# Where the sum of squares of a gated norm is issued: out of the output product, in between the next piece's products

## The chip, the core and the metric

The kernel runs on one core of a Trainium2 chip. Its engines are named as the profile names them: TensorE (PE, with its weight loads PEld), VectorE (DVE), ScalarE (ACT), GpSimd (POOL) and SyncE (SP). Each engine takes its instructions in the order in which the kernel issues them, and waits at an instruction until what it reads is there. The metric is the device time in microseconds of one execution.

## The reference

The input is 4 sequences of 1024 rows by 512. Four blocks are added to it, one after the other: a mixer ("a": 16 heads of 64, state 64), a feed-forward block, a second mixer ("b": 64 heads of 16, state 128), and the feed-forward block again with the same weights. Each block reads a layer-normalised copy of x. A mixer is a state-space layer:

```
proj = norm(x) @ in_proj            # z (1024), h (1024), B, C, dt (one per head)
h, B, C = silu(conv4(h, B, C))      # causal convolution, 4 taps
dt = softplus(dt + bias); decay per head = exp(dt * A)
y  = scan over time (state <- state*decay + dt*h*B; y = C.state) + D*h
a:  yf = y * silu(z);  out = (norm_w * yf * rsqrt(mean(yf^2) + eps)) @ out_proj
b:  out = (norm_w * y * rsqrt(mean(y^2) + eps) * silu(z)) @ out_proj
```

What matters here is the last line of each: the mean of 1024 squares for each row gives one factor a row. That factor commutes with the output product, so it can be put on the product's 512 outputs.

## The kernel before, in words

The kernel runs mixer a, the feed-forward block, mixer b and the feed-forward block in sequence. Within a mixer the rows are tiled by 128 (a chunk, 8 to a sequence), and two chunks form a group (256 rows); 16 groups follow each other. Matrix products are float32, and each is issued to PE as two passes, so that the profile counts each twice.

Two kinds of work are interleaved by hand. The *front* (`front`, L443) of the next group is a generator of pieces: `gate(n)` (four large products of 256 columns, for z) and `convolve(j)` (four large products of 259 columns, for h, B and C, with the four taps on ACT and DVE). The *chunk* (`chunk`, L763) does the scan of the present group: the masks and decays (`decays`, into tiles named seg and L), `weigh` (L813, a product with Gm on DVE), `inner` (L829, the products py), `close_y` (y, its square, its gate) and `to_state`. After each step a chunk yields a number of microseconds, which the loop at L1013 to L1023 adds to `due`; it then issues pieces, each with its own price (1.75 or 1.9), until `due` is used up. What a piece or a step leaves for a little later stands in `later_on`, which the loop empties behind the next piece (`waiting`) or at the end (`catch_up`).

A third list, `small`, holds small products: transposes of the normalised x (turn, L431), the dt projection (`project_dt`, L500, eight steps a group) and the 13 steps of a chunk's prologue (L697). `large` (L346) issues one large product and then one step of this list. `defer` puts steps at its end or, with `first=True`, at its head; `finish(part)` issues steps from the head until none of `part` is left. A front starts with `finish(xnT)` and puts its dt steps at the head; a chunk starts with `finish(f)`, which issues what is left of its prologue. In the last group there is no front any more, and the loop breaks off as soon as it finds no piece.

The end of a chunk runs inside the next one. `fold` (L970) adds the chunk's squares on DVE from 8 blocks of 128 columns to two; it is issued at the start of the next chunk. Behind the masks of that chunk, `tail` (L659) issues the output product: eight products of 512 columns into pout. The squares' sum, `ssq`, is a product of the two folded blocks with a column of ones; its two products are issued behind the seventh and the eighth product of pout. `leave`, by way of `later_on`, copies pout on ACT, computes mean plus eps (rs, L680) on DVE, and takes its power of -1/2 on POOL (`rsqrt`, L223). Then `from_state` issues po (L847), the chunk's share from the state. At the chunk's next step, behind weigh(L0) (and, in mixer b, the masks of weigh(L1)), the tail goes on: rs is scaled (L685), the product is added to x (L686), x is stored, and the statistics for the next block are taken.

In this text an even tail is that of a group's first chunk, which runs in the group's second; an odd tail is that of a group's second chunk, which runs in the next group's first, where a new front begins.

Of the kernel before, what the change touches and what calls it, by code (L numbers as in the profile page):

```python
# [12 lines left out]
ALU = mybir.AluOpType  # L13
# [7 lines left out]
E = 1024  # L21
KE = E // P
# [50 lines left out]
def hybrid_kernel(  # L73
# [37 lines left out]
    nc = tc.nc  # L111
# [38 lines left out]
    ones = const.tile([P, P], F32, tag="ones", name="ones")  # L150
# [35 lines left out]
    sums = [const.tile([P, SETS, HB, P], F16, tag=f"upto{i}", name=f"upto_{i}") for i in range(2)]  # L186

    def lay_constants():
        eye = ident.rearrange("p (r w) -> p r w", w=32)
        for i, at in enumerate(  # L190
            [slice(2 + h + 10 * lo, 7 + h + 10 * lo, 4) for lo in (0, 1) for h in range(HB)]
            + [slice(10 * lo, 10 * lo + 2) for lo in (0, 1)]
            + [slice(20, 21)]
        ):
            nc.vector.tensor_reduce(flags[:, i : i + 1], eye[:, :, at], mybir.AxisListType.XY, ALU.add)
        nc.vector.scalar_tensor_tensor(
            heads4, flags[:, HB : 2 * HB], 1.0 / LO_SCALE, heads4, ALU.mult, ALU.add
        )
        nc.vector.scalar_tensor_tensor(
            first2, flags[:, 2 * HB + 1 : 2 * HB + 2], 1.0 / LO_SCALE, first2, ALU.mult, ALU.add  # L200
        )
        for past in pasts:
            nc.vector.tensor_scalar_mul(
                past.rearrange("p t s -> p (t s)"), first2.to_broadcast([P, SETS * P]), -1.0
            )
            nc.vector.tensor_scalar(past[:, :, 64:], past[:, :, 64:], row20, None, ALU.add)

    def lay_flags(sets):
        for upto in sums:
            for t in sets:  # L210
                nc.vector.tensor_copy(upto[:, t], heads4.unsqueeze(2).to_broadcast([P, HB, P]))
                nc.vector.scalar_tensor_tensor(
                    upto[:, t, :, :64],
                    row20.unsqueeze(1).to_broadcast([P, HB, 64]),
                    MASKED,
                    upto[:, t, :, :64],
                    ALU.mult,
                    ALU.add,
                )

    def rsqrt(v):

        nc.gpsimd.tensor_tensor(v, v, neg_half[: v.shape[0]], ALU.pow)  # L223

    def layer_stats(pool, src, eps, tag, name, out=None):

        n = src.shape[0]
        st = pool.tile([P, 6], F32, tag=f"st_{tag}", name=f"st_{name}")
        nc.vector.bn_stats(st[:n], src)
        mv = pool.tile([P, 2], F32, tag=f"mv_{tag}", name=f"mv_{name}") if out is None else out  # L230
        nc.vector.bn_aggr(mv[:n], st[:n])
        nc.vector.tensor_scalar_add(mv[:n, 1:2], mv[:n, 1:2], eps)
        rsqrt(mv[:n, 1:2])
        return mv[:n]
# [12 lines left out]
    def mixer(m, in_w, conv_w, conv_b, dt_bias, A_log, Dv, norm_w, out_w, src, dst, first, stats, last_steps={}):  # L247
# [18 lines left out]
        with stack:  # L266
# [6 lines left out]
            def mm(name):  # L273
                return p_mm.tile([P, 512], F32, tag="mm", name=name)
# [8 lines left out]
            q = nc.scalar if first else nc.sync  # L283
# [53 lines left out]
            later_on = []  # L337

            def catch_up():
                while later_on:  # L340
                    later_on.pop(0)()


            small = []
# [6 lines left out]
            def finish(part):  # L351

                while any(p is part for p, _ in pending):
                    small.pop(0)()
# [3 lines left out]
            def defer(part, steps, first=False):  # L358

                runs = []  # L360
                for n, step in enumerate(steps):
                    last = n == len(steps) - 1
                    if last:
                        pending.append((part, None))

                    def run(step=step, last=last):
                        step()
                        if last:
                            pending[:] = [p for p in pending if p[0] is not part]

                    runs.append(run)
                small[:] = runs + small if first else small + runs
# [286 lines left out]
            def tail(f, c, sqs):  # L659

                i = f.b * NCH + f.g * GC + c
                tag = f"{m.name}_{i}"
                cols = slice(c * P, (c + 1) * P)


                pout = mm(f"pout_{tag}")
                ssq = mm(f"ssq_{tag}")
                for e in range(KE):
                    on = dict(start=(e == 0), stop=(e == KE - 1))
                    nc.tensor.matmul(pout, f.hs[e // 2][:, e % 2, cols], w_out[:, e, :], **on)  # L670
                    if e >= KE - 2:
                        nc.tensor.matmul(
                            ssq[:, 0:1], sqs[0][:, e - KE + 2, :], ones[:, 0:1], start=(e == KE - 2), stop=(e == KE - 1)
                        )
                po = wk.tile([P, D], F32, tag="t2k", name=f"out_{tag}", bufs=4)
                rs = sm.tile([P, 1], F32, tag="rs", name=f"rs_{tag}", bufs=1)

                def leave():
                    nc.scalar.copy(po, pout)  # L679
                    nc.vector.tensor_scalar(rs, ssq[:, 0:1], 1.0 / E, m.eps, ALU.mult, ALU.add)  # L680
                    rsqrt(rs)

                later_on.append(leave)
                yield
                nc.vector.tensor_scalar_mul(rs, rs, gc)  # L685
                nc.vector.scalar_tensor_tensor(f.xs[c], po, rs, f.xs[c], ALU.mult, ALU.add)  # L686
                later_on.append(lambda: nc.scalar.dma_start(dst[i], f.xs[c]))

                layer_stats(sm, f.xs[c], 1e-5, "g", f"g{tag}", out=stats[:, i, 0:2])
                later_on.append(  # L690
                    lambda: nc.vector.scalar_tensor_tensor(
                        stats[:, i, 2:3], stats[:, i, 0:1], -1.0, stats[:, i, 1:2], ALU.mult, ALU.mult
                    )
                )
                yield
# [285 lines left out]
            with tc.manual_schedule(  # L981
                engines={
                    mybir.EngineType.PE,
                    mybir.EngineType.DVE,
                    mybir.EngineType.Activation,
                    mybir.EngineType.Pool,
                }
            ):
                fs = [Group(*groups[0]), Group(*groups[1])]
                for _ in norm(fs[0], None):  # L990
                    pass
                if first:
                    lay_constants()
                    lay_flags(range(TS))
                weighing = weigh_rows()
                for at, _ in enumerate(front(fs[0], fs[1])):
                    catch_up()
                    if at >= 6:
                        next(weighing, None)
                for _ in weighing:  # L1000
                    pass
                lay_sums(fs[0], 0)
                if first:
                    lay_flags(range(TS, SETS))
                for n in range(len(groups)):
                    if n + 2 < len(groups):
                        fs.append(Group(*groups[n + 2]))
                    f, ahead, behind = (fs + [None, None])[n : n + 3]
                    pieces = front(ahead, behind) if ahead is not None else iter(())
                    due = 0.0  # L1010
                    for c in range(GC):
                        following = (f, c + 1) if c + 1 < GC else (None if ahead is None else (ahead, 0))
                        for us in chunk(f, c, following):  # L1013
                            due += us
                            while due > 0.0:
                                waiting, later_on[:] = later_on[:], []
                                piece = next(pieces, None)
                                for step in waiting:
                                    step()
                                if piece is None:  # L1020
                                    break
                                due -= piece
                            catch_up()  # L1023
                    for _ in pieces:
                        catch_up()
                state.pop("fold")()
                for _ in state["tail"]:
                    catch_up()
# [438 lines left out]
```

## Time and profile before

| | us |
|---|---|
| median of 3 runs | 3059.65 (3053.1 to 3065.45) |
| the profiled execution | 3044.65 |
| its span | 3042.9 |
| PE busy, share | 2767.9, 91% |
| DVE busy, share | 2081.7, 68% |
| ACT busy, share | 1261.8, 41% |
| POOL busy, share | 720.3, 24% |
| mean granted clock of PE | 0.963 |
| mixer a, steady part | about 100 to 1102 |
| mixer b, steady part | about 1430 to 2756 |

A row of the waits names who waited for whom, then the total in us, the number of times and the longest. A row of the timeline has the start in us from the span's start, the length, the engine, the line and the operation, out<-in by the program's names, and in brackets the idle time before it and what ended that. A row of the windows has the stretch, its length, the busy time of each engine with the number of instructions, and at its end PEclk, the clock granted to PE as a share of full speed, the share of the DMA engines and GB/s.

### The profile page before, as it was taken

To read this page: it belongs to the slowest core of one execution; us is meant where nothing else is said; L and a number is where in the kernel's file an instruction comes from. 1 tells how busy PE (TensorE), PEld (TensorE's weight loads), DVE (VectorE), ACT (ScalarE), POOL (GpSimd) and SP (SyncE) were. 2 spreads that over 40 slices of the span, in tenths; PEclk is the share of its full clock that TensorE was granted. 3 is DMA by queue.
4 is the path that set the end of the run, shared out by engine and by line. 5 is a ranking of instruction groups with operands and counts; after the bars stand their busy time and mean duration, and the time that the engine had idled before them with its cause. 6 is when DMAs were issued, how large, how long until landed. Compare 5 with 4: busy or idle time off the path is not lost. (4 is left out here: it accounts for less than half of the span.)

```text
span 3042.9 us, 46127 instructions
## 1 busy us (share of the span) xinstructions
PE 2767.9 (91%) x17156; PEld 1789.5 (59%) x17156; DVE 2081.7 (68%) x4417; ACT 1261.8 (41%) x2874; POOL 720.3 (24%) x839
## 2 busy tenths in 40 slices
PE   7999999999999988999999899999888888898986
PEld 5666666666666653456666666666555565564332
DVE  5667666766666662477777687776787777875368
ACT  3334433334333332355444444444444444443245
POOL 1222122122212221351111112212222222212057
PEclk8999999999999999999999999999999999998999
DMA  3000000000000015430000000000000000001423
GB/s 117 14 19 16 16 16 17 24 17 17 16 17 22 10 68 205 154 102 10 17 20 20 13 20 18 13 17 21 22 25 21 20 23 20 13 11 72 170 88 110
DMA packets 92959, 124.25 MB, mean 41 GB/s; under 512 B 38728, under 2 KB 42328, under 8 KB 92736
## 3 DMA queue, kind: packets, MB, share of 16 engines
q1 hardware_dynamic: 80960, 98.23, 10.0%
q10 hardware_dynamic: 9792, 16.82, 1.5%
q0 software_dynamic: 1984, 6.26, 0.6%
q8 instruction: 136, 2.23, 0.3%
q14 instruction: 87, 0.71, 0.1%
HBM read 84.54 MB, written 36.72 MB: 40 GB/s over the span
## 5 line engine op out<-in xcount | busy, mean ns | idle before, releaser
L347 PE MATMUL pc_b<-xnT_b,w_in_b 128*128 128x259 f32 x1280 | 355.7, 408 | 25.1 <-DVE S_b L909 21.9
L813 DVE TENSOR_TENSOR L_b<-L_b,Gm_b 128x1024 f32<-128x1024 f32 x256 | 308.7, 1247 | 2.9 <-ACT L_b L806 2.9
L347 PE MATMUL pz_a<-xnT_a,w_in_a 128*128 128x256 f32 x1024 | 296.5, 408 | 2.9 <-ACT Bt_a L756 2.3
L347 PE MATMUL pc_a<-xnT_a,w_in_a 128*128 128x259 f32 x1152 | 299.1, 394 | 0.0
L806 ACT ACTIVATE L_b<-seg_b 128x512 f32<-128x512 f32 x512 | 263.6, 603 | 74.0 <-PE seg_b L799 74.0
L347 PE MATMUL pz_b<-xnT_b,w_in_b 128*128 128x256 f32 x1024 | 291.4, 397 | 2.9 <-ACT xnT_b L436 2.9
L474 DVE SCALAR_TENSOR_TENSOR u_b<-pc_b,cw_b,u_b 128x256 f32<-128x256 f32 x480 | 231.5, 482 | 79.8 <-ACT u_b L470 68.3
L347 PEld LDWEIGHTS pc_b<-xnT_b,w_in_b 128*128 128x128 f32 x1280 | 229.3, 198 | 92.7 <-DVE S_b L909 25.4
L474 DVE SCALAR_TENSOR_TENSOR u_a<-pc_a,cw_a,u_a 128x256 f32<-128x256 f32 x432 | 208.2, 482 | 73.6 <-ACT u_a L470 63.3
L1205 PE MATMUL g_ps<-gw,xnT_f 128*128 128x512 f32 x512 | 246.9, 619 | 9.6 <-DMA gw<-in_L_ffn_gate_w 4.2
L829 PE MATMUL py_b<-L_b,hdt_b 128*32 128x128 f32 x4096 | 165.7, 299 | 97.6 <-DVE L_b L813 96.5
L670 PE MATMUL pout_a<-w_out_a,h_a 128*128 128x512 f32 x512 | 240.2, 613 | 0.0
L670 PE MATMUL pout_b<-w_out_b,h_b 128*128 128x512 f32 x512 | 235.7, 604 | 0.0
L347 PEld LDWEIGHTS pc_a<-xnT_a,w_in_a 128*128 128x128 f32 x1152 | 200.9, 190 | 58.5 <-DVE rs_a L685 11.4
L882 POOL TENSOR_TENSOR h_b<-h_b,z_b 128x256 f32<-128x256 f32 x128 | 90.8, 730 | 509.5 <-ACT sq_b L881 509.5
L347 PEld LDWEIGHTS pz_a<-xnT_a,w_in_a 128*128 128x128 f32 x1024 | 172.3, 195 | 55.0 <-ACT out_a L679 14.4
L347 PEld LDWEIGHTS pz_b<-xnT_b,w_in_b 128*128 128x128 f32 x1024 | 174.5, 194 | 48.8 <-issue 26.0
L829 PEld LDWEIGHTS py_b<-L_b,hdt_b 128*32 128x32 f32 x4096 | 112.6, 117 | 147.7 <-DVE L_b L813 60.5
L1205 PEld LDWEIGHTS g_ps<-gw,xnT_f 128*128 128x128 f32 x512 | 93.2, 196 | 122.1 <-issue 113.5
L881 ACT ACTIVATE sq_b<-h_b 128x256 f32<-128x256 f32 x128 | 47.9, 417 | 262.5 <-DVE h_b L878 262.5
L670 PEld LDWEIGHTS pout_a<-w_out_a,h_a 128*128 128x128 f32 x512 | 93.3, 192 | 100.1 <-issue 96.3
L670 PEld LDWEIGHTS pout_b<-w_out_b,h_b 128*128 128x128 f32 x512 | 92.3, 190 | 99.5 <-issue 95.7
(321 smaller groups left out, 4919.7 us busy)
## 6 DMA issues: line engine op xcount, KB each, us to landing
d<-in_L_ffn_d_w SPq DMA_DIRECT2D x4, 2048.0 KB
x_f<-xa SPq DMA_DIRECT2D x32, 256.0 KB
xb<-x_b ACTq DMA_DIRECT2D x32, 256.0 KB
x_f<-xb SPq DMA_DIRECT2D x32, 256.0 KB
x_a<-in_L_attn_a_x SPq DMA_DIRECT2D x30, 256.0 KB
xa<-x_a ACTq DMA_DIRECT2D x30, 256.0 KB
out<-x_f SPq DMA_DIRECT2D x22, 256.0 KB
xf<-x_f SPq DMA_DIRECT2D x20, 256.0 KB
```

The source lines that it names most:

```text
L347: nc.tensor.matmul(*args, **kw)
L474: nc.vector.scalar_tensor_tensor(u, ps[:, k : k + GT], cw[:, j, k : k + 1], u, ALU.mult, ALU.add)
L670: nc.tensor.matmul(pout, f.hs[e // 2][:, e % 2, cols], w_out[:, e, :], **on)
L806: nc.scalar.activation(L[:, r], sg[r0 + r], AF.Exp)
L813: nc.vector.tensor_mul(Lr, Lr, Gm.unsqueeze(1).to_broadcast([P, 2 * HB, P]))
L829: nc.tensor.matmul(py[cg * CT : (cg + 1) * CT, e % 4, :], hdt[:, h // HC, u : u + HC, :], Ls[half][:, r, hq, :], start=not started[cg], st ...
L881: nc.scalar.activation(sr, yh, AF.Square)
L882: nc.gpsimd.tensor_mul(yh, yh, zs[half * 2 + r][:, :, cols])
L1205: nc.tensor.matmul(ps, xnT[:, k, :], gw[:, k, :], start=(k == 0), stop=(k == KD - 1 and not bias_on_pe))
```

## The change

The two ssq products leave the pout chain. They become two steps at the head of `small`, so that they are issued behind large products of the next piece; the second of them puts `leave` into `later_on`. `leave` no longer copies pout; that copy stands in `later_on` by itself, as before. Where the tail goes on, `finish(rs)` issues the two steps if they have not been issued, and `leave` is called if it has not run (its list `sums` has a second entry once it has).

The loop that hands out pieces no longer breaks off where it finds no piece: it issues steps of `small`, each counted as 0.35 us, until `due` is used up or `small` is empty. That concerns the last group of each mixer, and the last step of other groups where the pieces have run out.

```diff
                 pout = mm(f"pout_{tag}")
-                ssq = mm(f"ssq_{tag}")
                 for e in range(KE):
                     on = dict(start=(e == 0), stop=(e == KE - 1))
                     nc.tensor.matmul(pout, f.hs[e // 2][:, e % 2, cols], w_out[:, e, :], **on)
-                    if e >= KE - 2:
-                        nc.tensor.matmul(
-                            ssq[:, 0:1], sqs[0][:, e - KE + 2, :], ones[:, 0:1], start=(e == KE - 2), stop=(e == KE - 1)
-                        )
                 po = wk.tile([P, D], F32, tag="t2k", name=f"out_{tag}", bufs=4)
                 rs = sm.tile([P, 1], F32, tag="rs", name=f"rs_{tag}", bufs=1)
 
+                sums = []
+
+                def add_squares(q):
+                    if q == 0:
+                        sums.append(mm(f"ssq_{tag}"))
+                    nc.tensor.matmul(sums[0][:, 0:1], sqs[0][:, q, :], ones[:, 0:1], start=(q == 0), stop=(q == 1))
+                    if q == 1:
+                        later_on.append(leave)
+
                 def leave():
-                    nc.scalar.copy(po, pout)
-                    nc.vector.tensor_scalar(rs, ssq[:, 0:1], 1.0 / E, m.eps, ALU.mult, ALU.add)
-                    rsqrt(rs)
-
-                later_on.append(leave)
+                    if len(sums) == 1:
+                        nc.vector.tensor_scalar(rs, sums[0][:, 0:1], 1.0 / E, m.eps, ALU.mult, ALU.add)
+                        rsqrt(rs)
+                        sums.append(None)
+
+                defer(rs, [lambda q=q: add_squares(q) for q in range(2)], True)
+                later_on.append(lambda: nc.scalar.copy(po, pout))
                 yield
+                finish(rs)
+                leave()
                 nc.vector.tensor_scalar_mul(rs, rs, gc)
                 nc.vector.scalar_tensor_tensor(f.xs[c], po, rs, f.xs[c], ALU.mult, ALU.add)
...
                                 if piece is None:
+
+                                    if small:
+                                        small.pop(0)()
+                                        due -= 0.35
+                                        continue
                                     break
                                 due -= piece
```

## The prediction

> **What bounds the kernel now.** I read the page's busy shares first, then the waits of TensorE alone, once for mixer a (100 to 1100 us) and once for mixer b (1440 to 2760 us).
>
> ```profile
> span 3042.9 us, 46127 instructions
> ...
> PE 2767.9 (91%) x17156; PEld 1789.5 (59%) x17156; DVE 2081.7 (68%) x4417; ACT 1261.8 (41%) x2874; POOL 720.3 (24%) x839
> ```
>
> TensorE (PE) is busy for 91%, so what it waits for is what can be won. Its waits in mixer a (us in total, times, longest):
>
> ```profile
> PE ssq_a L672 <- DVE sq_a L972: 28.8, 14, 2.7
> PE py_a L860 <- DVE h_a L878: 7.9, 15, 1.0
> PE py_a L829 <- DVE h_a L878: 1.2, 3, 0.4
> ```
>
> and in mixer b:
>
> ```profile
> PE py_b L829 <- DVE L_b L813: 83.3, 61, 5.8
> PE pc_b L347 <- DVE S_b L909: 21.9, 12, 2.2
> PE ssq_b L672 <- DVE sq_b L972: 4.3, 5, 1.7
> ```
>
> In mixer a the wait that the change moves is three quarters of all; mixer b waits for VectorE's weighing (L813) instead. Next the timeline of PE at one of the 14 waits, and VectorE's (DVE) beside it:
>
> ```profile
> 654.82 1.02 PE L670 MATMUL pout_a<-w_out_a,h_a 128*128 128x512 f32 x2
> 658.58 0.35 PE L672 MATMUL ssq_a<-ones,sq_a 128*128 128x1 f32 x2 [2.74 <-DVE sq_a L972]
> 658.80 1.84 PE L670 MATMUL pout_a<-w_out_a,h_a 128*128 128x512 f32 x2
> ...
> 660.78 1.94 PE L847 MATMUL po_a<-S_a,Cc_a 64*128 64x512 f32 x4
> 662.65 0.70 PE L347 MATMUL pz_a<-xnT_a,w_in_a 128*128 128x256 f32 x2
> ```
>
> ```profile
> 657.29 0.68 DVE L971 TENSOR_TENSOR sq_a<-sq_a,sq_a 128x512 f32<-128x512 f32 x1
> 658.01 0.42 DVE L972 TENSOR_TENSOR sq_a<-sq_a 128x256 f32<-128x256 f32 x1
> 662.75 1.29 DVE L851 TENSOR_TENSOR yo_a<-po_a,ea_a 128x512 f32<-128x512 f32 x2 [4.32 <-PE po_a L847]
> ```
>
> The ssq product stands inside the pout chain and holds the two last pout passes, po and the next piece until the fold (L971, L972) is done; DVE then idles 4.32 us for po. So each engine waits for the other in turn. The windows' PEclk after the wait (third figure from the right):
>
> ```profile
> 655.00:658.50 3.50, 0.84 (x2) 0.01 (x1) 3.23 (x10) 1.53 (x4) 0.00 (x0) 1.00 0.00 0
> 658.50:662.60 4.10, 4.02 (x10) 1.70 (x10) 0.00 (x0) 0.58 (x1) 0.00 (x0) 0.58 0.00 0
> ```
>
> After the idle time the granted clock is halved for some 3.4 us, while PE is busy.
>
> **The change part by part.** One profiled execution: 3044.65 us, span 3042.9. It lies 15 us under the median of 3059.65; I carry the difference over to that median.
>
> 1. *The two products leave the pout chain.* In an undisturbed tail pout passes start 0.43 us apart, and ssq0 to ssq1 is 1.08 us (1919.86 to 1920.95 in mixer b) with two pout passes between: an ssq costs 0.22 us, 0.44 a tail. Between large products the nearest row is the dt step (L503), also two passes: large and step together take 0.65 us (1923.49 to 1924.14), a large alone 0.43. Again 0.22. Net zero on PE.
>
> 2. *The even tails* (of a group's first chunk, run in its second). Pieces are under way, so the two steps stand first in the list and go behind the first and second large product of the next gate piece. Ahead of ssq0 there is now the last pout product (2 x 0.43), po (453.27 to 454.33, 1.06 us in an undisturbed clock) and one large product (0.43): 2.35 us more work. The wait is 2.74 us as idle time and 2.90 from start to start (658.58 - 655.25 - 0.43), 0.16 more; 14 waits then cost 28.8 + 14 x 0.16 = 31.0 us. Three of them (379, 659, 936 us) are 2.90 and keep 0.55 each: 1.65. Gain 29.4 us. The fold does not move, since DVE works without a gap before it. What comes late next is yo: it can start at 658.44 at the earliest, about 1 us behind po; DVE has 1.41 us idle later, at z (L541, waiting for ACT's tanh at 667.97), and that hides it. Without that cover 1 us x 14 comes back.
>
> 3. *The clock behind these waits.* Windows at half clock (0.51) follow seven of the 14: five of 3.5 us, two of 6.9 (379.1 and 935.5), 31.3 us in all, in which PE works at half speed: 31.3 x 0.49 = 15.3 us. Bounds: nothing, if the windows come elsewhere; 20 us, the whole shortfall of mixer a (mean clock 0.98 over 1002 us). As every one begins within a us of an ssq wait's end, I take 15.3.
> The Trainium skill ("TensorE: Matmul & The Clock Gate", section "Why this matters for your kernels") sets the limit for a drop to half clock at idle gaps of about 3 us; the seven waits that one follows are 1.8 to 2.7 us, so by the page none of these windows is due to them, this term is nil, and the sum is the first rival's. The trace disagrees with the page: seven windows sit right behind such waits.
>
> 4. *Mixer b's even tails.* Five waits, 4.3 + 5 x 0.16 = 5.1 us, all under 2.35, and one half-clock window (2341.8 to 2345.3 us): 1.7. Gain 6.8.
>
> 5. *The odd tails* (of a group's second chunk, run in the next group's first). There the next piece opens a new front, which puts its eight dt steps ahead of the list; two gate pieces have just eight large products. The ssq steps are left over and are issued by finish(rs) behind weigh(L0), with rs, the root on POOL and the scaling directly behind each other on DVE. The same chain is seen at the mixer's end:
>
> ```profile
> 1153.67 0.16 DVE L680 TENSOR_SCALAR rs_a<-ssq_a 128x1 f32<-128x1 f32 x1 [4.72 <-PE ssq_a L672]
> 1154.49 0.15 DVE L685 TENSOR_SCALAR rs_a<-rs_a 128x1 f32<-128x1 f32 x1 [0.66 <-POOL rs_a L223]
> ```
>
> Now the scaling starts at once behind the weighing, as the root was taken six us before:
>
> ```profile
> 1929.41 2.35 DVE L813 TENSOR_TENSOR L_b<-L_b,Gm_b 128x1024 f32<-128x1024 f32 x2
> 1931.68 0.15 DVE L685 TENSOR_SCALAR rs_b<-rs_b 128x1 f32<-128x1 f32 x1
> ```
>
> ```profile
> 1937.57 0.64 PE L829 MATMUL py_b<-L_b,hdt_b 128*32 128x128 f32 x16 [0.36 <-DVE L_b L813]
> ```
>
> So DVE gets 0.66 + 0.15 = 0.81 us more before the layer statistics, u (L474) and weigh(L1), for which PE already waits in mixer b. Against it, po and both gates come 0.44 us sooner, and with them z and weigh(L0). Net 0.37 us in each of 14 groups: a loss of 5.2 us. The products themselves are in time: PE issues them behind the masks of weigh(L1) (1928.17 to 1929.05), while weigh(L0) runs to 1931.68. POOL's queue is empty there (its scaling of S ended at 1925.1). Bounds: -0.44 (the root hidden) to +0.81, -6.2 to +11.3 us. In mixer a PE waits for nothing in the 24 us behind these scalings and DVE idles 0.84 us for ACT (L470): nothing, at most 14 x 0.81 = 11.3 if that cover is gone.
>
> 6. *rs and root in the even tails* go behind one more piece, but still before weigh(L0), 2.35 us long, against 0.81 for the chain; POOL has only S's scaling (1.04 in a, 1.93 in b) ahead. Nothing; 0.66 a tail if the cover is gone. The copy of pout keeps its place in ACT's queue. No DMA is added; the store of x behind a late scaling has no reader before the feed-forward stage.
>
> 7. *Filling in the last group.* The 13 prologue steps of the last chunk go from its start into the waits of the chunk before. They take 4.2 us in mixer a (1120.39 to 1124.59, at half clock) and 2.0 in b (2777.44 to 2779.46), while PE waited 4.27 us in the chunk before in a. But DVE, which sets that chunk's end, takes over 0.29 + 2 x 0.68 = 1.65 us. Gain 4.2 - 1.65 = 2.5 in a; in b 2.0 less a part of 1.65 (DVE has a gap of 1.36 there): 1. Bounds 0 and 6.2. At the end of mixer a's other groups the same loop issues six steps that finish(f) would have issued next; on ACT four scalings (L727, 0.29 each) get ahead of the exponentials, with 7 us of pout to hide them. Nothing.
>
> Sum: -29.4 - 15.3 - 6.8 + 5.2 - 2.5 - 1 = -49.8 us: 2995 for the profiled execution, 3010 for the median.
>
> **The rivals.**
> *A. The clock windows stay*, elsewhere: the clock also halves without these waits (mixer b's mean is 0.96). Then terms 3 and 4 lose 17 us: -33, 3027. For: windows hit only seven of 14 waits; against: between these seven windows mixer a's clock is 1.00 from 106 to 1102 us. This is the case that the page's limit would give.
> *B. Given back on DVE.* Every odd tail costs the full 0.81 us in both mixers (28 x 0.81 = 22.7 for 5.2) and the clock stays too: -33 + 17.5 = -15.5: 3044, no change. For: mixer b already waits for DVE; against: DVE's idle time in mixer a.
> *C. Slower: the ssq tile's bank.* In the odd tails its PSUM tile is now taken after weigh(L0) has been queued. If its bank is one that DVE frees only behind that weighing, PE stands for 2.35 us, and rs 0.81 after it: 3.2 x 28 = 88 us against the 55 of the other terms: +33, 3093. It decides from (55 + 15) / 28 = 2.5 us a tail. Against: seven banks, and the tiles ahead of it are read before the weighing.
> *D. The steps do not move the wait:* ssq0 behind the first large product waits as long as before. That would need the fold to come 2.35 us later; it hangs on ACT and DVE alone. Only terms 5 and 7 are left, +1.7: 3061, counted with B.
>
> **How the numbers follow.** Forecast 0.62, A 0.20, B with D 0.11, C 0.07. A measurement of this kernel tells 0.5% (15 us) from no change: faster 0.82, same 0.11, slower 0.07. The time is the forecast's, 3010. Low end: term 5 at -6.2 instead of +5.2, the last groups at -6.2 instead of -3.5, the clock at -20 instead of -15.3: 18.8 us less, 2991, rounded to 2990. High end: B's 3044, beyond which lie D and C.
>
> **What the next profile would show.** Right: no wait of ssq_a for sq_a above 0.6 us and under 3 us in all; PEclk 1.00 behind the even tails; yo_a's idle time for po shorter; DVE's L685 idle 0.66 us for POOL in 28 odd tails; py_b's wait for L_b up by 5 to 11 us. Wrong: a wait of some 2 us at the ssq in the gate piece (D), a PE wait ahead of ssq in the odd tails (C), half-clock windows without ssq waits (A).

## The result, and the profile after

The changed kernel takes 3012.67 us (median of 4 runs, 3010.38 to 3019.51) against 3056.38 before (4 runs): a ratio of 0.9856, 95% interval 0.9828 to 0.9885, or 44 us less. The forecast was 50 us less.

The page of the profile after, its first lines:

```profile
span 3010.1 us, 46168 instructions
...
PE 2761.4 (92%) x17156; PEld 1785.4 (59%) x17156; DVE 2085.2 (69%) x4417; ACT 1259.9 (42%) x2874; POOL 721.1 (24%) x839
```

The same work, in a shorter span. TensorE's waits in the steady part of mixer a (us in total, times, longest):

```profile
PE py_a L868 <- DVE h_a L886: 11.6, 26, 1.0
PE ssq_a L678 <- DVE sq_a L980: 2.9, 3, 1.0
```

and in mixer b:

```profile
PE py_b L837 <- DVE L_b L821: 96.2, 76, 5.3
PE pc_b L347 <- DVE S_b L917: 16.7, 12, 2.2
```

The wait for the fold has shrunk from 28.8 to 2.9 us in mixer a and is gone from mixer b's list. Two others have grown: py_a's for h_a, from 15 times to 26, and py_b's for L_b, by 13 us. Not all of the latter belongs to the change: over the 28 tails of mixer b it is 83.3 us before and 95.0 after, but 90.8 in a run below that leaves mixer b as it was (the one with added products). The same even tail as in the prediction, now on PE:

```profile
640.99 2.31 PE L669 MATMUL pout_a<-w_out_a,h_a 128*128 128x512 f32 x5
643.23 1.13 PE L855 MATMUL po_a<-S_a,Cc_a 64*128 64x512 f32 x4
644.29 0.70 PE L347 MATMUL pz_a<-xnT_a,w_in_a 128*128 128x256 f32 x2
645.95 0.35 PE L678 MATMUL ssq_a<-ones,sq_a 128*128 128x1 f32 x2 [0.96 <-DVE sq_a L980]
```

pout runs through, po follows at once, and the first ssq stands behind one large product. The granted clock (third figure from the right) over mixer a's steady part, before and after:

```profile
100.00:1102.00 1002.00, 964.15 (x5177) 0.98 0.06 17
```

```profile
106.00:1073.00 967.00, 950.19 (x5176) 1.00 0.06 18
```

Cut at the first pass of each chunk's pout, the two traces can be laid beside each other stretch by stretch. Each stretch holds one tail:

| stretches | forecast, us | measured, us | time at half clock in them |
|---|---|---|---|
| mixer a, 14 even tails | -44.7 | -41.1 | 30.7 -> 0 |
| mixer a, 14 odd tails | 0 | +6.5 | 0 -> 0 |
| mixer a, last group | -2.5 | -4.1 | 15.1 -> 10.9 |
| mixer b, 14 even tails | -6.8 | -15.8 | 34.1 -> 20.5 |
| mixer b, 14 odd tails | +5.2 | +10.7 | 64.9 -> 75.1 |
| mixer b, last group | -1.0 | -2.9 | 16.8 -> 10.2 |
| sum | -49.8 | -46.6 | |

The last group of a mixer is three stretches here, up to the output product of its last chunk. That the two sums lie 3 us apart is in part luck: mixer a's even tails and the odd tails of both mixers came out 15.6 us worse than forecast, mixer b's even tails and the two last groups 12.5 us better.

The two spans differ by only 32.8 us, since the profiled execution of before reached its first pout after 94.0 us and that of after needed 100.2. That is scatter: of the runs below in which the squares' sum stays inside the output product, the one with a late root needed 102.0 us, the one with the filling alone 101.2, and the one with two added products 94.5. The feed-forward blocks scatter by 2 to 6 us likewise.

### The profile page after: what moved, and what is told of

It is laid out like the page before. It is cut to its first block, busy times and chain, and to the rows that moved or that the text cites. A ratio compares the mean times of both kernels' runs of the same rounds, so it can differ in the third digit from the quotient of the medians.

```text
span 3010.1 us, 46168 instructions
## 1 busy us (share of the span) xinstructions
PE 2761.4 (92%) x17156; PEld 1785.4 (59%) x17156; DVE 2085.2 (69%) x4417; ACT 1259.9 (42%) x2874; POOL 721.1 (24%) x839
## 3 DMA queue, kind: packets, MB, share of 16 engines
q1 hardware_dynamic: 80960, 98.23, 10.2%
## 5 line engine op out<-in xcount | busy, mean ns | idle before, releaser
L347 PE MATMUL pz_a<-xnT_a,w_in_a 128*128 128x256 f32 x1024 | 303.5, 410 | 3.0 <-ACT Bt_a L764 2.3
L347 PE MATMUL pz_b<-xnT_b,w_in_b 128*128 128x256 f32 x1024 | 298.7, 402 | 3.2 <-ACT xnT_b L436 3.2
L669 PE MATMUL pout_a<-w_out_a,h_a 128*128 128x512 f32 x512 | 230.3, 603 | 0.0
L669 PE MATMUL pout_b<-w_out_b,h_b 128*128 128x512 f32 x512 | 228.3, 599 | 0.0
```

What stands on the lines that cost most here:

```text
L347: nc.tensor.matmul(*args, **kw)
```

## The experiments

All of them are compared by the median time, with before run on the same chip, and by the stretches above. The first four below ran on one chip, the changed kernel once more among them; the last four ran on another, where the changed kernel was not run.

**The changed kernel once more.** It was run to tell what belongs to the change from scatter.

> The changed kernel once more, beside the other runs of this chip: 0.983 to 0.989 of before. Its profile shows whether the 6.2 us that the stretch ahead of the first output product took longer than before (100.2 against 94.0 us), and the 5.8 us of the feed-forward block between the mixers, belong to the change: if they do they are there again within 1 us; if they are scatter of the start and of the clock they are not.

3012.34 us, ratio 0.9852 (0.9827 to 0.9876). First pout at 102.4 us, the stretch between the mixers 285.2 (287.9 in the first profile, 282.1 before): scatter. Mixer a's tails repeat within 0.15 us. In mixer b a stretch changes by up to 1.6 us, always where a half-clock window fell elsewhere: mixer b's odd tails have 71.7 us at half clock here.

**TensorE kept busy during the wait.** The fold is waited for as before, but not idly.

```diff
                 for e in range(KE):
                     nc.tensor.matmul(pout, f.hs[e // 2][:, e % 2, cols], w_out[:, e, :], **on)
+                    if e == KE - 2 and m.name == "a" and c == 0:
+                        for _ in range(2):
+                            nc.tensor.matmul(ssq, ident, w_out[:, 0, :], start=True, stop=True, ...)
```

> The kernel before, but in mixer a's even tails TensorE issues two more 512-column products (1.72 us, their result is overwritten) between the seventh output product and ssq0, so that it is busy for most of the wait for the fold; nothing else moves. Theory (the half-clock windows are set off by these idle times): the waits shrink to 0.6 to 1.2 us, the half-clock windows between 100 and 1102 us go, and the time falls by 13 to 15 us although the fold is waited for as long as before; the three tails that waited 1.34 us lose 0.4 us each. Rival (the clock falls by itself): the windows stay, the time is within 2 us of before.

3045.30 us, ratio 0.9965 (0.9949 to 0.9981): 11 us less, with more work, where 13 to 15 had been expected. The waits that are left, and the clock between 100 and 1102 us:

```profile
PE ssq_a L675 <- DVE sq_a L975: 5.5, 10, 0.9
```

```profile
100.00:1102.00 1002.00, 986.35 (x5273) 1.00 0.06 20
```

The windows are gone. The five tails that were followed by a single window are 1.62 to 1.72 us shorter, the two with a double one 2.23 and 3.01; together 13.6 us. In the tail of 2.23 TensorE stood 0.85 us longer at the last masks for a DMA (`past`), which no other of these tails did; without that its windows were worth 3.08, and all of them 14.5. The four that waited 2.34 us without a window are within 0.06 us of before, and the three that waited 1.34 us are 0.3 longer. So the half clock behind these waits was set off by them and cost some 14 us in the profiled execution. The rival, that the clock falls by itself, is out for mixer a.

**The root late, the sum where it was.** This is the VectorE chain of the odd tails alone.

```diff
                 def leave():
-                    nc.scalar.copy(po, pout)
...
-                later_on.append(leave)
+                odd = c == 1 and f.g * GC + c + f.b * NCH < NT - 3
+                later_on.append(lambda: nc.scalar.copy(po, pout))
+                if not odd:
+                    later_on.append(leave)
                 yield
+                if odd:
+                    leave()
```

> The kernel before, but in the 28 odd tails with a new front the mean (rs) and the root are issued right ahead of the scaling, behind weigh(L0); the ssq products stay inside the output product. This measures the chain on VectorE by itself. Theory: VectorE idles 0.66 us for POOL in each and the whole 0.81 us reaches TensorE in mixer b (11 us) and 0.8 to 0.9 us a tail in mixer a too (12 us): 20 to 25 us slower. Rival (mixer a hides it, as the prediction had it): 11 us slower, mixer a's odd tails unchanged at 34.13 us.

3085.54 us, ratio 1.0092 (1.0070 to 1.0114): 29 us slower, more than the 20 to 25 expected. Mixer a's odd tails are longer by 0.82 to 0.84 us, every one of the 14. Ahead of the scaling DVE stood idle for POOL in mixer a (us, times):

```profile
  POOL rs_a L223: 9.9, 15
```

0.66 us each, and with rs itself (0.15) the 0.81 us of the prediction. On PE the wait shows where the second half of y waits for the first half's buffer (py_a for h_a), and it is more frequent, as in the changed kernel:

```profile
PE py_a L864 <- DVE h_a L882: 15.4, 24, 1.0
```

Mixer b's odd tails cost 18.8 us more in all, 13.6 us more at half clock among them, which is worth 6.8; the other 12.0 are 0.86 a tail. An odd tail with no half clock in either profile went from 45.77 to 46.61 us, 0.84 more. The rival, that mixer a hides the chain, is out.

**The sum ahead of the dt steps.** If the chain is what the odd tails lose, the order in the list of small products mends it.

```diff
-                small[:] = runs + small if first else small + runs
+                at = sum(1 for s in small if getattr(s, "sums", False)) if first else len(small)
+                for r in runs:
+                    r.sums = first == "sums"
+                small[at:at] = runs
...
-                defer(rs, [lambda q=q: add_squares(q) for q in range(2)], True)
+                defer(rs, [lambda q=q: add_squares(q) for q in range(2)], "sums")
```

> The changed kernel, but the dt steps are put behind the two ssq steps in the list of small products, so that in the odd tails too the sum is taken behind the first and second large product of the next piece, and the root on POOL is done before weigh(L0) ends. Theory (the odd tails lose time through the chain rs, root, scaling on VectorE): the 14 odd tails of mixer a, each 0.49 us longer in the changed kernel than before, return to 34.13 us or less, VectorE's idle time of 0.66 us ahead of the scaling is gone in all 28, mixer b gains 0.4 to 1 us in each odd tail: 10 to 20 us less than the changed kernel in all. Rival (they lose because the two products are placed together ahead of the next convolution, or because of the clock): odd tails stay 0.4 us or more longer than before, total within 4 us of the changed kernel.

2998.78 us, ratio 0.9810 (0.9793 to 0.9828), against 0.9852 (0.9827 to 0.9876) for the changed kernel on the same chip: the fastest of all, 14 us less than the changed kernel. In the profiles the odd tails lost 5.5 us in mixer a and 4.6 in mixer b, 0.33 a tail there, where 0.4 to 1 had been expected. Another 3.3 us are in mixer b's even tails, which have 10 us less at half clock and which the new order does not touch. Mixer a's waits:

```profile
PE py_a L871 <- DVE h_a L889: 7.9, 15, 1.0
PE ssq_a L681 <- DVE sq_a L983: 2.9, 3, 1.0
```

py_a's wait is back at the 7.9 us, 15 times, of before, and DVE's idle time for POOL ahead of the scaling is down to the one at the mixer's end. Mixer a's odd tails fell from +0.49 to +0.16 against before. They did not return to before as I had expected: ten large products are needed for ten steps, two gate pieces have eight, and so the second chunk's dt addition slips behind the weighing and onto DVE's chain:

```profile
684.95 0.15 DVE L696 TENSOR_SCALAR rs_a<-rs_a 128x1 f32<-128x1 f32 x1
...
686.94 0.17 DVE L514 TENSOR_TENSOR v_a<-pd_a,dtb_a 128x16 f32<-128x16 f32 x1
```

**Both products right behind po.** This changes the cover ahead of ssq0 by one large product.

```diff
-                defer(rs, [lambda q=q: add_squares(q) for q in range(2)], True)
+                state["squares"] = lambda: [add_squares(q) for q in range(2)]
...
-                finish(rs)
...
                     from_state()
+                state.pop("squares", lambda: None)()
...
```

> The changed kernel with the two products placed right behind po in every tail, ahead of the next piece, and not in the list of small products. This tests the cover: ahead of ssq0 there are the last output product and po, 1.92 us, in place of 2.35 us. Theory: in mixer a's even tails the waits of 2.34 us keep 0.42 us and those of 2.90 keep 1.0 or a little more: 5 to 7 us more than the changed kernel in these; the odd tails have the root done early, VectorE has no idle time of 0.66 us, and mixer a's odd tails fall back from +0.49 to 0: 7 us less. Rival for the even tails: the large product is no cover at all, because the fold and not TensorE sets the time: they stay as in the changed kernel.

3010.86 us, ratio 0.9858 (0.9835 to 0.9882): the same as the changed kernel, from two halves that cancel. Mixer a's even tails took 5.1 us more than in the changed kernel, its odd ones 4.9 us less. The waits for the fold:

```profile
PE ssq_a L678 <- DVE sq_a L980: 6.6, 10, 1.6
```

The tails of 2.34 us keep 0.29 to 0.34 us, where 0.42 was expected, and those of 2.90 that kept 1.0 us lose 0.43 and 0.44 more; in one of these a window came back, which makes 2.14. So the large product was cover, and the fold sets the rest.

**Behind po in the odd tails alone.** The same lines as above, under `if c == 1`.

> The changed kernel with the two products right behind po in the odd tails alone, in the even tails as in the changed kernel. Theory: even tails as in the changed kernel (2.3 us less than before and more where a window went), mixer a's odd tails at 0 against before (0.49 in the changed kernel, 0.16 with the sums ahead of the dt steps, where the dt addition of the second chunk slips behind weigh(L0)), no 0.66 us of idle time ahead of the scaling: 10 to 18 us less than the changed kernel, 0 to 5 us less than with the sums ahead of the dt steps. Rival: the 0.16 us is the price of the products outside the output product and stays.

3001.99 us, ratio 0.9829 (0.9807 to 0.9851): 7 us less than the changed kernel by the ratios, 10 by the medians, on another chip and with intervals that overlap (0.9807 to 0.9851 here, 0.9827 to 0.9876 there), and level with the sums ahead of the dt steps. Mixer a's odd tails are at +0.11 against before, not at 0. So a tenth of a microsecond a tail stays, and the rival holds for it. On TensorE, in one of these tails (the 18th stretch), the two products right behind po take 0.47 us, while po without them starts only 0.34 us sooner behind the first pass of pout (7.06 us for 7.40). The next piece starts 0.13 us later (8.59 for 8.46), and DVE's z 0.11 us later (14.59 for 14.48).

**The filling taken out, and the filling alone.**

```diff
                                 if piece is None:
-                                    if small:
-                                        small.pop(0)()
-                                        due -= 0.35
-                                        continue
                                     break
```

> The changed kernel with the loop breaking off again where it finds no piece, so without filling. Theory: all but the last groups stays as in the changed kernel; the last group of mixer a (from the output product of its first chunk to that of its last, 20.9 us in the changed kernel, 25.1 before) goes back to 25 us and mixer b's to 31: 5 to 6 us slower than the changed kernel. Rival: the shorter last groups come from the moved products themselves, and stay.

3020.88 us, ratio 0.9888 (0.9865 to 0.9911). Against the changed kernel mixer a's last group is 5.2 us longer and mixer b's 4.8, with 13.5 us more at half clock in b's, worth some 7, more than the whole difference. All other stretches of mixer a are the same, but for one. Mixer b's odd tails are 8.2 us longer in this profile, with 17 us more at half clock.

> The kernel before with the filling alone; the squares' sum stays inside the output product. Theory: even and odd tails as before within 0.1 us except for half-clock windows, the last groups 4 and 1.6 us shorter: 5 to 6 us faster than before, 0.2%, within the scatter of the total. Rival: the six steps issued earlier at the end of mixer a's other groups cost ScalarE's queue something: odd tails longer.

3053.17 us, ratio 0.9991 (0.9973 to 1.0009), no difference in the total. The last groups are 3.1 and 2.1 us shorter, and all but one of the odd tails of mixer a are as before within 0.01 us: issuing six steps earlier there costs nothing, and that rival is out. The rival of the run without filling is out for mixer a, whose last group is as long as before again (1.1 us longer). In mixer b, and for the size of the gain in both, the clock in the last groups leaves it open.

## Why the prediction was right, step by step

*Step 1 (net zero on PE)* held to a tenth of a microsecond a tail. PE's busy time went from 2767.9 to 2761.4 us, but less of it was at half clock, so that this alone shows little. In mixer a's odd tails po starts 0.34 us sooner, and the two products cost 0.44 later on.

*Step 2 (the even tails' waits)* held in its mechanism: the tails of 2.34 us without a window gained 2.30 to 2.31 us, those of 1.34 us 1.26 to 1.33. The three longest kept 0.96 us of idle time, 1.12 from start to start, not 0.55, so that the sign "no wait above 0.6 us" failed. "The fold does not move" was wrong there by 0.8 us: it ends 9.63 us behind the first pass of pout, where it ended at 8.87. As po now comes earlier, POOL's scaling of S runs beside the fold. VectorE and POOL in that tail:

```profile
643.90 0.69 DVE L979 TENSOR_TENSOR sq_a<-sq_a,sq_a 128x512 f32<-128x512 f32 x1
644.62 1.18 DVE L980 TENSOR_TENSOR sq_a<-sq_a 128x256 f32<-128x256 f32 x1
```

```profile
644.48 1.04 POOL L936 TENSOR_TENSOR S_a<-S_a,ea_a 128x512 f32<-128x512 f32 x1 [8.26 <-PE po_a L855]
```

The second addition took 1.18 us in place of 0.42. In the same tails of the run with added products, where po and the scaling come later, it took 0.42, and likewise in the tails of 2.34 us, whose fold is over before the scaling starts.

*Step 3 (the clock)* was right in kind and a little too large: 14.5 us, or 13.6 with the DMA's delay, for 15.3. Most of the rest is in the two double windows, in which PE was not busy throughout: 6.39 and 6.29 us of 6.9.

*Step 4 (mixer b's even tails)* was too small, 6.8 for 15.8, and the step left something out. Six tails of the second half gave 7.9 us; five of them are those with a wait. The four that had no window in either profile gained 0.49 to 0.54 us beyond their wait, which fits po's standing 0.44 us earlier in a mixer where PE waits for DVE anyway. The other eight tails never waited for the fold, and the prediction put them at nothing; they gave 7.8 us. Without half clock such a tail takes 42.10 us where mixer b is as before (the run with added products), and 41.29 to 41.43 in the changed kernel. The order on ACT shows why. The two ssq steps take the places of two transposes in the list of small products, and the copy of the transposes (L436) no longer stands ahead of the tanh for z (L536). Mixer b's eleventh output product with both products behind po, and in the changed kernel:

```profile
1861.49 0.59 ACT L436 COPY xnT_b<-tpx_b 128x512 f32<-128x512 f32 x1 [9.34 <-PE tpx_b L434]
1861.97 0.60 ACT L536 ACTIVATE tz_b<-pz_b 128x512 f32<-128x512 f32 x1
```

```profile
1856.44 0.60 ACT L536 ACTIVATE tz_b<-pz_b 128x512 f32<-128x512 f32 x1 [9.01 <-PE pz_b L347]
```

Counted from the first pass of pout that is 11.99 and 11.17 us, and z on DVE moves from 12.62 to 11.91. With both products behind po, po is just as early, but the order on ACT is the old one and the tail takes 42.17 us; so here it is not po that gives the gain. Whether the 13.6 us less at half clock belong to the change is not shown: with mixer b untouched its even tails have 34.1 us at half clock in one profile and 17.1 in another.

*Step 5 (the odd tails)* failed for mixer a, where I wrote "nothing" on the ground that PE waited for nothing behind these scalings and DVE idled 0.84 us for ACT (L470). The chain was there as described, DVE first and PE after it:

```profile
684.95 2.35 DVE L821 TENSOR_TENSOR L_a<-L_a,Gm_a 128x1024 f32<-128x1024 f32 x2
687.22 0.15 DVE L684 TENSOR_SCALAR rs_a<-ssq_a 128x1 f32<-128x1 f32 x1
688.04 0.15 DVE L693 TENSOR_SCALAR rs_a<-rs_a 128x1 f32<-128x1 f32 x1 [0.66 <-POOL rs_a L223]
```

```profile
696.90 0.63 PE L868 MATMUL py_a<-ident,yo_a 128*128 128x128 f32 x4 [0.34 <-DVE h_a L886]
```

The cover was none. DVE's 0.84 us of idle time are still there in all 14 odd tails, in the changed kernel and with the late root alone:

```profile
692.44 0.20 ACT L762 ACTIVATE ea_a<-misc_a 128x40 f32<-128x40 f32 x1 [4.75 <-DVE Gm_a L760]
693.25 1.52 DVE L474 SCALAR_TENSOR_TENSOR u_a<-pc_a,cw_a,u_a 128x256 f32<-128x256 f32 x3 [0.84 <-ACT u_a L470]
```

ACT issues u_a (L470) behind ea_a, which waits for DVE's Gm_a (L760). When DVE is late, ACT is late by as much, and the idle time moves along and takes up nothing. An absent wait on PE was no measure of slack either: the late root alone, 0.81 us on DVE, made each tail 0.83 us longer. Of this the changed kernel gets 0.33 back, because z starts that much sooner behind the first pass of pout (14.15 us for 14.48), which leaves the 0.49.

In mixer b the net price was right: 10.7 us less 5.1 for the clock is 0.40 a tail, for 0.37 forecast. The subtraction is rough, since with mixer b untouched (the run with added products) the odd tails are 5.4 us longer than before at the same 64.9 us at half clock; but the one odd tail with no half clock in either profile agrees, 45.77 us before and 46.16 after. The chain alone cost 0.83 and 0.86 us in the two mixers, for 0.81.

*Step 6 (the even tails' root)* held; only the odd tails, and the mixers' ends, show DVE's idle time for POOL (15 times in each mixer).

*Step 7 (filling)* was a little small: 4.1 and 2.9 us in the first profile, 3.1 and 2.1 by itself, for 2.5 and 1, each with 3 to 7 us less at half clock among them.

Rival A fell for mixer a with the busy wait: its windows did not come elsewhere. In mixer b there is less half clock in the even tails and more in the odd ones; whether the windows moved or only fell otherwise is not shown. Rival B had the right place and, in mixer a, half of the full price, but the even tails won too much for it to decide. C did not happen: PE's masks wait 2.0 us for rs_b in mixer b, 6 times, where before pc_b waited 3.2 us for it, 6 times. Nor did D.

## What to carry to other kernels

A product that waits for another engine inside a chain should go behind work that does not depend on it, and the cover can be added up beforehand from the rows of the trace. Then look at who else stands in the list it joins: here the gain in half of the tails was partly paid back because eight other steps came first, and a change of order took another 14 us off, some 10 of them in the odd tails that it touches. Idle time of an engine is cover only if what ends it does not itself hang on the work that comes late. A wait of some two microseconds on TensorE costs its own length and may cost as much again in clock.

## What the runs showed of the hardware that I had not expected

In each of the ten profiles the half-clock windows begin on a grid of 3.413 us. The prediction quoted the Trainium skill ("TensorE: Matmul & The Clock Gate", section "Why this matters for your kernels") for a limit of about 3 us of idle time. The same page of the Trainium skill (section "Part 1: The HAM clock gate (the "warmup" mystery)") gives free-running windows of 3413 ns, and with that the traces agree; with the limit they do not. Four windows of the grid before the change, TensorE alone (stretch, length, busy time with instructions, clock):

```profile
655.62:659.03 3.42, 0.68 (x4) 1.00 0.00 0
659.03:662.45 3.42, 3.42 (x8) 0.50 0.00 0
448.25:451.65 3.40, 1.47 (x4) 1.00 0.00 0
451.65:455.07 3.42, 3.16 (x13) 1.00 0.00 0
```

With 2.74 us idle in one window the next ran at half clock; a wait of 2.18 us that fell across a border of the grid left 1.93 idle in the first and set nothing off. Over the ten profiles, between 100 and 2750 us, a window at full clock with 2.0 us of idle time or more was always followed by half a clock, one with under 1.37 us never; between these both occur. So, as far as these traces go, what counts is the idle time within a window of the grid, and the same wait costs 1.7 us more or nothing, by where it falls: of mixer a's seven waits of 2.18 us before the change, three were followed by a window and four were not. That mixer b, with 23 waits of 2 us and more in its 28 tails before the change, changes by several microseconds from one execution to the next fits this, but was not tested by itself.
